# A graph layer on one core: the first gather of each group waits for TensorE, tables are moved in halves, and the sum goes first on VectorE

## The chip, the cores and the metric

The kernel runs on one core of one Trainium2 chip. The metric is the device time of one execution in microseconds. Before the change three runs gave a median of 1374.2 us (1370.36 to 1376.34).

The engines of the core are called by the names that the profile uses: PE is TensorE (matmuls; PEld is its weight loads), DVE is VectorE, ACT is ScalarE, POOL is GpSimd, and SP is SyncE, which here only issues transfers. The engines run their own instruction lists and wait for each other by semaphores.

## The reference

One message-passing layer on a graph with N = 6250 nodes of H = 128 features and E = 100000 edges with ED = 4 features each. The edges come sorted by their destination. All numbers are float32.

```python
msg_in = concatenate([x[src], x[dst], edge_attr], axis=1)      # 100000 x 260
h = silu(msg_in @ mW1 + mb1)                                   # 100000 x 128
messages = h @ mW2 + mb2
aggregated = segment_sum(messages, dst, num_segments=N)        # 6250 x 128
u = silu(concatenate([x, aggregated], axis=1) @ uW1 + ub1)
updated = u @ uW2 + ub2
y = layer_norm(x + updated, ln_g, ln_b)
out = layernorm(x + y)
```

## The kernel before, in words

**Factoring.** The first product is split by its rows: `x[src] @ mW1[:128]` is a row of the table `tab_a = x @ mW1[:128]`, and `x[dst] @ mW1[128:256] + mb1` is a row of the table `tab_b`. Both tables are made once, in an opening stage, and written to DRAM. Since the sum over edges is linear, `mW2` is applied to the nodes' sums of `h` rather than to the edges.

**Tiling.** An edge tile has P = 128 edges. G = 8 tiles make a group of GE = 1024 edges, and there are NG = 98 groups. As the edges are sorted by destination, the destinations of a group lie in a window of W = 96 consecutive nodes, whose first node is `bases[g]`. The nodes are NT = 49 tiles of 128.

**Work on one group g.** The names are those of the functions in the code.

- `fetch(g)` issues eight indirect transfers from GpSimd (L268), each of which collects 128 rows of 512 bytes by the source indices. The rows come out of `tab_a`, or, for the first RAW groups, out of `x` itself, as the table is not there yet. The buffers of the pool `gath` are AHEAD + 2 = 6, so the gathers of group g wait until the rows of group g - 6 are used.
- `load(g)` brings 96 rows of `tab_b` from the group's window into `mv`, and four rows of edge features into the lower rows of `st`. The last four rows of `mv` are the edge part of `mW1`.
- `node_matrix(g)` (L527, VectorE) writes the one-hot matrix window x edges into the upper 96 rows of `st`, and counts the edges of each node on the way.
- `products(g)` (L552, TensorE) does eight matmuls `st^T mv`. Their result `pre` (in PSUM, three buffers) is the part of `x[dst]` and of the edge features, for each edge.
- `hidden(g)` adds the gathered rows and `pre` on VectorE (the sum `s`, L570), and takes the silu on ScalarE (L571). For a raw group it turns the gathered rows of `x` on TensorE first, copies them, and multiplies them by the first half of `mW1` inside `products`.
- `edge_matrix(g)` (L540, VectorE) makes the one-hot matrix edges x window, `oh`.
- `by_nodes(g)` turns the counts (L577) and does eight matmuls `h^T oh` (L580, TensorE), which sum the hidden rows of the group by node, into the tile `held_ps`.
- `add(g)` (L586, VectorE) adds that to `acc`, features x nodes, in SBUF, and the counts to `deg`.

**Batches of nodes.** When the edges of four node tiles are complete, a `node_batch` does the rest for these nodes: two matmul stages, silu, two normalisations. It is written as a generator, and one of its steps is done at the end of each pass of the loop. There are 12 batches and one last one, about one for every eight groups.

**Order.** For SP, TensorE, VectorE and ScalarE the order of the instructions is the order of the code, by hand (`manual_schedule`). GpSimd is not in that list, and a scheduler places its gathers. In pass g the code does, in this order: `fetch(g + 4)`, `load(g + 4)`, `node_matrix(g + 3)`, `products(g + 2)`, `hidden(g)`, `edge_matrix(g + 1)`, `by_nodes(g - 1)`, `add(g - 2)`, and a step of the running batch. So on VectorE a pass is node_matrix, sum, oh, add. The tile `held_ps` is one tile for all its uses: it also holds the row of window numbers that `edge_matrix` reads. In the program as built, L577 of by_nodes(g - 1) therefore waits for `oh` of group g + 1 of the same pass, and `add(g - 2)` waits for by_nodes(g - 1) of the same pass. On VectorE the chain of a pass is then sum, oh, (by_nodes on TensorE), add, the batch's step, and the node_matrix and the sum of the next pass.

**The opening.** The gathers of the first RAW = 5 groups are issued ahead of everything else on GpSimd, 40 in number. Then the tables are made in `parts` of eight node tiles, seven parts in all, the last of one tile. For each part, TensorE turns the rows of `x` (`turn_x`) and multiplies each turned tile by the two halves of `mW1` in two calls of `product` (L322, eight matmuls of 128 columns each). VectorE moves the result of `tab_b` out of PSUM and adds the bias (L338), ScalarE moves that of `tab_a` (L341). Each is followed by a transfer of 512 KB to DRAM. The gathers of group RAW, the first from the table, wait for the transfers of all parts.

Of the kernel before, what the change touches and what calls it, by code (L numbers as in the profile page):

```python
# [8 lines left out]
F32 = mybir.dt.float32  # L9
# [9 lines left out]
P = 128  # L19
# [5 lines left out]
def kernel(  # L25
# [40 lines left out]
    nc = tc.nc  # L66
    N, H = x.shape
# [4 lines left out]
    G = 8  # L72
    GE = G * P
    NG = -(-E // GE)
# [4 lines left out]
    RB = 14  # L79
    AHEAD = 4  # L80
    LEAD = 4
    RAW = 5
    MADE = 3
    NQ = 4
    NM = 5
# [11 lines left out]
    def groups(n, g):  # L97
        return [(i, min(g, n - i)) for i in range(0, n, g)]
# [13 lines left out]
    def wide():  # L112
        return ps.tile([P, G, P], F32, name="pre", bufs=3)
# [5 lines left out]
    tpool = tables.enter_context(tc.tile_pool(name="tables", bufs=1, side="right"))  # L119
# [25 lines left out]
    x_sb = tpool.tile([P, NT, H], F32, name="x_sb")  # L145
    nf = N // P
    w1 = consts.tile([P, 2, H], F32, name="w1")
    src_l = by_group(src, 0)
    nc.scalar.dma_start(w1, mW1[: 2 * H].rearrange("(s k) f -> k s f", k=P))
    b1 = consts.tile([P, H], F32, name="b1")  # L150
# [11 lines left out]
    mv = [consts.tile([K1, H], F32, name=f"mv{k}") for k in range(NM)]  # L162
# [91 lines left out]
    tab_a = dram.tile([NP, H], F32, name="tab_a")  # L254
    tab_b = dram.tile([NW, H], F32, name="tab_b")
    ea_d = dram.tile([ED, NG * GE], F32, name="ea_d")
    near_d = dram.tile([NG, GE], U8, name="near_d")
    rows, bases, near = {}, {}, {}

    def tiles_of(g):  # L260
        return min(G, -(-(E - g * GE) // P))

    def fetch(g):
        if g >= NG:
            return
        rows[g] = gath.tile([P, G, H], F32, name="ga")
        for i in range(tiles_of(g)):
            nc.gpsimd.indirect_dma_start(  # L268
                out=rows[g][:, i, :],
                out_offset=None,  # L270
                in_=x if g < RAW else tab_a[:, :],
                in_offset=bass.IndirectOffsetOnAxis(
                    ap=src_i[:, g, i : i + 1] if g else src_0[:, i : i + 1], axis=0
                ),
            )

    for g in range(RAW):
        fetch(g)
# [30 lines left out]
    xT = consts.tile([P, NP], F32, name="xT")  # L309

    def by_node(t):
        return t[:NP].rearrange("(i p) f -> p i f", p=P)
# [2 lines left out]
    nc.vector.memset(zeros, 0.0)  # L315
    nc.sync.dma_start(tab_b[NP:NW], zeros)

    def product(i0, n, part):
        pm = wide()
        for i in range(n):  # L320
            cols = slice((i0 + i) * P, (i0 + i + 1) * P)
            nc.tensor.matmul(pm[:, i, :], xT[:, cols], w1[:, part, :], start=True, stop=True)  # L322
        return pm[:, :n]

    def turn_x(i0, n):
        pt = wide()
        for i in range(n):
            nc.tensor.transpose(pt[:, i, :], x_sb[:, i0 + i, :], ident)
        nc.scalar.copy(xT[:, i0 * P : (i0 + n) * P], pt[:, :n, :].rearrange("p i f -> p (i f)"))
# [3 lines left out]
    for k, (i0, n) in enumerate(parts):  # L333
        if k + 1 < len(parts):
            turn_x(*parts[k + 1])

        t = x_sb[:, i0 : i0 + n, :]
        nc.vector.tensor_add(t, product(i0, n, 1), b1[:, None, :].to_broadcast([P, n, H]))  # L338
        nc.sync.dma_start(by_node(tab_b)[:, i0 : i0 + n, :], t)
        t = tpool.tile([P, G, H], F32, name="t", bufs=2)  # L340
        nc.scalar.copy(t[:, :n], product(i0, n, 0))  # L341
        nc.sync.dma_start(by_node(tab_a)[:, i0 : i0 + n, :], t[:, :n])
        cols = slice(i0 * P, NW if i0 + n == NT else (i0 + n) * P)
        nc.vector.memset(acc[:, cols], 0.0)
        nc.vector.memset(deg[:, cols], 0.0)
# [23 lines left out]
    def load_weights():  # L369
        for name, shape in (("w2", [P, H]), ("u1a", [P, H]), ("mb2", [P, 1])):  # L370
            raw_w[name] = work.tile(shape, F32, name=f"raw_{name}", bufs=1)
        nc.sync.dma_start(raw_w["w2"], mW2)
        nc.sync.dma_start(raw_w["u1a"], uW1[P:])
        nc.sync.dma_start(raw_w["mb2"], mb2.rearrange("(f o) -> f o", o=1))
        nc.sync.dma_start(u1x, uW1[:P])
        nc.sync.dma_start(u2, uW2)
        nc.sync.dma_start(ub1_col, ub1.rearrange("(f o) -> f o", o=1))
        nc.sync.dma_start(ub2_row, ub2.rearrange("(o f) -> o f", o=1))
        for t, row in ((g_b, ln_g), (b_b, ln_b)):
            nc.sync.dma_start(t, row.rearrange("(o f) -> o f", o=1).to_broadcast([P, H]))  # L380

    def fuse_weights():
        pt = narrow()
        nc.tensor.transpose(pt[:, :P], raw_w["w2"], ident)
        w2T = work.tile([P, P], F32, name="w2T", bufs=1)
        nc.scalar.copy(w2T, pt[:, :P])
        pm = narrow()
        nc.tensor.matmul(pm[:, :H], w2T, raw_w["u1a"], start=True, stop=True)
        nc.tensor.matmul(pm[0:1, H:], raw_w["mb2"], raw_w["u1a"], start=True, stop=True)
        nc.scalar.copy(w2u, pm[:, :H])  # L390
        nc.scalar.copy(mb2u, pm[0:1, H:])
# [133 lines left out]
    def node_matrix(g):  # L525

        nc.vector.tensor_scalar(  # L527
            stbuf[g % NST][:W],
            near.pop(g),
            p_next,  # L530
            0.0,
            op0=OP.is_equal,
            op1=OP.add,
            accum_out=deg_g[:, g : g + 1],
        )

    def edge_matrix(g):

        oh = work.tile([P, G, W], F32, name="oh", bufs=3)
        nc.vector.tensor_tensor(  # L540
            oh,
            w_row[:, None, :].to_broadcast([P, G, W]),
            rel[:, g, :, None].to_broadcast([P, G, W]),
            op=OP.is_equal,
        )
        return oh

    def products(g, xg=None):
        pre = wide()
        st = stbuf[g % NST].rearrange("k (i c) -> k i c", i=G)  # L550
        for i in range(tiles_of(g)):
            nc.tensor.matmul(pre[:, i, :], st[:, i, :], mv[g % NM], start=True, stop=xg is None)  # L552
            if xg is not None:
                nc.tensor.matmul(pre[:, i, :], xg[:, i, :], w1[:, 0, :], start=False, stop=True)  # L554
        return pre

    def hidden(g):
        h = hbuf[g % NH]
        ga = rows.pop(g)
        if g < RAW:  # L560
            px = wide()
            for i in range(G):
                nc.tensor.transpose(px[:, i, :], ga[:, i, :], ident)
            xg = work.tile([P, G, P], F32, name="s")
            nc.vector.tensor_copy(xg, px)  # L565
            nc.scalar.activation(h, products(g, xg), AF.Silu)
        else:
            n = tiles_of(g)
            s = work.tile([P, G, H], F32, name="s")
            nc.vector.tensor_add(s[:, :n], ga[:, :n], pre.pop(g)[:, :n])  # L570
            nc.scalar.activation(h[:, :n], s[:, :n], AF.Silu)  # L571
        return h
# [19 lines left out]
    pre, oh, h, pt, running = {}, {0: edge_matrix(0)}, {}, {}, []  # L592
    for g in range(NG + 1):
        if g == 3:
            load_weights()
        if g == 5:
            fuse_weights()
        for c in range(1, NC):
            if g == max(1, c * EC // GE - 10):
                attributes(c)  # L600
            if g == max(1, c * EC // GE - 10) + 1:
                attribute_rows(c)
        if g + AHEAD >= RAW:
            fetch(g + AHEAD)
        if g + LEAD < NG:
            load(g + LEAD)
        if g + MADE < NG:
            node_matrix(g + MADE)
        if g >= RAW:
            for k in range(g if g == RAW else g + MADE - 1, min(g + MADE, NG)):  # L610
                pre[k] = products(k)
        if g < NG - 1:
            h[g] = hidden(g)
        if g + 1 < NG:
            oh[g + 1] = edge_matrix(g + 1)
        if 0 <= g - 1 < NG:
            pt[g - 1] = by_nodes(g - 1, h.pop(g - 1), oh.pop(g - 1))
        for k in range(max(g - 2, 0), g - 1 if g < NG - 1 else g):
            if k in pt:
                add(k, pt.pop(k))  # L620
        for i0, n, first in batches:
            if g == min(first + 1, NG):
                tiles = node_tiles(nodes, node_ps)
                if first == NG:

                    tiles = (
                        nodes,
                        lambda name, p=P: gath.tile([P, G, H], F32, name="ga")[:p, :BT],
                        lambda: wide()[:, :BT],
                    )  # L630
                running.append(node_batch(i0, n, *tiles))
        advance(running)
        if g >= NG - 2:
            advance(running)
        if g == NG - 1:
            h[g] = hidden(g)
# [157 lines left out]
```

## Time and profile before

The profiled execution has a span of 1372.6 us and a mean granted TensorE clock of 0.665 of full speed.

| Engine | busy us | share | instructions |
|---|---|---|---|
| PE | 704.8 | 51% | 3818 |
| DVE | 477.5 | 35% | 1012 |
| ACT | 237.4 | 17% | 288 |
| POOL | 741.4 | 54% | 790 |

| Group of instructions | count | mean ns |
|---|---|---|
| gather L268 | 742 | 946 |
| products L552 | 1564 | 336 |
| sums by node L580 | 1564 | 361 |
| node_matrix L527 | 98 | 1262 |
| sum L570 | 93 | 1204 |
| add L586 (of acc) | 98 | 255 |

| Stage | us from the start of the span |
|---|---|
| gathers of groups 0 to 4 | 4.06 to 54.15 |
| tables' work on TensorE ends | 83.5 |
| first gather from a table | 88.99 |
| sums of groups 5 to 97 | 167.98 to 1346.93 |
| last gather | 1297.96 |

A mean duration times a count is the busy time of a group of instructions. Busy time is not what sets the end where engines wait for each other, and the profile names for each group what ended the idle time before it, the releaser: "DVE s L570" is the instruction of line 570 on VectorE that writes `s`; "issue" is time without a wait that the profile shows; "remote" is a wait whose end the profile can't lay at the end of any instruction that it shows. The durations of matmuls are modelled.

### The profile page before, as it was taken

What the parts mean: (1) busy time and instruction counts of PE and PEld (TensorE: products, weight loads), DVE (VectorE), ACT (ScalarE), POOL (GpSimd) and SP (SyncE); (2) the same over time, 40 slices, a digit from 0 to 9 for tenths busy, and PEclk for the clock granted to TensorE, in tenths of its full rate; (3) what the DMA queues carried; (4) which work ended last, traced back from release to release, by engine and by line L of the source; (5) the groups of instructions that cost most, each with busy time, mean ns of one, the idle gap of its engine ahead of it and who ended that gap; (6) DMA issues with size and microseconds to landing.
All of it is one profiled execution on the core that took longest, in us unless ns stands there. A gap on an engine that the chain in (4) does not pass through costs nothing. (4 is left out here: it accounts for less than half of the span.)

```text
span 1372.6 us, 11511 instructions
## 1 busy us (share of the span) xinstructions
PE 704.8 (51%) x3818; PEld 624.6 (46%) x3818; DVE 477.5 (35%) x1012; ACT 237.4 (17%) x288; POOL 741.4 (54%) x790
## 2 busy tenths in 40 slices
PE   3356743656465355445344543675543664544565
PEld 2356643545355244345234443565433454434453
DVE  1172323324334234234233325234324333225343
ACT  0121101112212112112102201212202202202223
POOL 7435564656456556546645654666655565655400
PEclk8577775755666657656656765656756665766765
DMA  6363222212312222222212221322222222222100
GB/s 168 90 177 83 56 66 65 64 48 57 79 43 67 55 60 70 58 57 70 74 33 68 56 64 41 78 58 74 62 58 58 56 69 64 58 58 56 47 1 28
DMA packets 69917, 88.96 MB, mean 65 GB/s; under 512 B 20671, under 2 KB 51534, under 8 KB 69850
## 3 DMA queue, kind: packets, MB, share of 16 engines
q0 software_dynamic: 25024, 51.30, 15.0%
q1 hardware_dynamic: 41290, 35.08, 9.0%
q10 hardware_dynamic: 3536, 1.77, 0.5%
q8 instruction: 32, 0.52, 0.1%
q14 instruction: 35, 0.29, 0.1%
HBM read 76.71 MB, written 11.38 MB: 64 GB/s over the span
## 5 line engine op out<-in xcount | busy, mean ns | idle before, releaser
L268 POOL DMA_INDIRECT ga<-tab_a,src_i x742 | 702.2, 946 | 541.6 <-DVE s L570 277.8
L552 PE MATMUL pre<-mv,st 100*128 100x128 f32 x1564 | 278.3, 336 | 57.2 <-issue 56.9
L586 DVE TENSOR_TENSOR acc<-acc,held_ps 128x96 f32 x98 | 25.0, 255 | 780.6 <-remote 511.7
L577 PE MATMUL held_ps<-ident,deg_g 96*1 96x96 f32 x98 | 28.6, 292 | 509.6 <-DVE oh L540 482.5
L552 PEld LDWEIGHTS pre<-mv,st 100*128 100x128 f32 x1564 | 257.6, 250 | 69.2 <-issue 68.8
L580 PE MATMUL held_ps<-oh,h 128*128 128x96 f32 x1564 | 287.5, 361 | 0.3 <-ACT h L571 0.3
L580 PEld LDWEIGHTS held_ps<-oh,h 128*128 128x128 f32 x1564 | 276.6, 274 | 1.4 <-ACT h L571 0.7
L577 PEld LDWEIGHTS held_ps<-ident,deg_g 96*1 96x1 f32 x98 | 8.0, 82 | 532.3 <-DVE oh L540 501.9
L571 ACT ACTIVATE h<-s 128x1024 f32<-128x1024 f32 (+1 forms) x93 | 98.1, 1055 | 718.4 <-DVE s L570 653.3
L527 DVE TENSOR_SCALAR_CACHE_REDUCE st<-near,p_next 96x1024 f32<-96x1024 uint8 x98 | 123.5, 1262 | 24.0 <-issue 14.3
L570 DVE TENSOR_TENSOR s<-ga,pre 128x1024 f32<-128x1024 f32 (+1 forms) x93 | 112.0, 1204 | 2.9 <-PE pre L552 2.7
L540 DVE TENSOR_TENSOR oh<-held_ps,rel 128x768 f32<-128x768 f32 x98 | 92.3, 942 | 0.0
L571 ACT ACT_TABLE_LOAD x21 | 26.9, 1283 | 126.0 <-DVE s L570 113.1
L322 PE MATMUL pre<-w,xT 128*128 128x128 f32 x196 | 29.1, 307 | 31.6 <-issue 15.7
L322 PEld LDWEIGHTS pre<-w,xT 128*128 128x128 f32 x196 | 27.4, 222 | 33.5 <-issue 16.0
L268 POOL DMA_INDIRECT ga<-in_x_dram,src_i x32 | 30.3, 946 | 9.8 <-issue 9.8
L554 PE MATMUL pre<-w,s 128*128 128x128 f32 x80 | 22.1, 371 | 18.9 <-DVE s L565 16.3
L417 ACT ACT_TABLE_LOAD x24 | 30.8, 1283 | 2.7 <-DVE mv L412 2.3
L446 PEld LDWEIGHTS y<-u,uT 128*128 128x128 f32 x94 | 22.7, 327 | 15.4 <-issue 15.4
L425 ACT COPY acc_b<-acc 128x512 f32<-128x512 f32 (+1 forms) x12 | 7.3, 609 | 124.3 <-DVE acc L586 115.3
L554 PEld LDWEIGHTS pre<-w,s 128*128 128x128 f32 x80 | 17.8, 275 | 19.9 <-DVE s L565 17.0
L446 PE MATMUL y<-u,uT 128*128 128x128 f32 x94 | 26.0, 448 | 0.0
(117 smaller groups left out, 396.0 us busy)
## 6 DMA issues: line engine op xcount, KB each, us to landing
ga<-tab_a,src_i POOLq DMA_INDIRECT x742
near<-near_d SPq DMA_DIRECT2D x24, 384.0 KB
mv<-tab_b SPq DMA_DIRECT2D x98, 48.0 KB
tab_b<-x_sb SPq DMA_DIRECT2D x6, 512.0 KB
tab_a<-t SPq DMA_DIRECT2D x6, 512.0 KB
xs<-in_x_dram SPq DMA_DIRECT2D x11, 256.0 KB
out_dram<-z SPq DMA_DIRECT2D x11, 256.0 KB
st<-ea_d SPq DMA_DIRECT2D x98, 16.0 KB
```

The source lines that it names most:

```text
L268: nc.gpsimd.indirect_dma_start(out=rows[g][:, i, :], out_offset=None, in_=x if g < RAW else tab_a[:, :], in_offset=bass.IndirectOffsetOnAx ...
L322: nc.tensor.matmul(pm[:, i, :], xT[:, cols], w1[:, part, :], start=True, stop=True)
L417: nc.scalar.activation(r[:, :n], mv[:, :n, 1], AF.Sqrt, bias=eps)
L446: nc.tensor.matmul(y[:, i, :], by_p[:, :, i], u2, start=False, stop=i == n - 1)
L527: nc.vector.tensor_scalar(stbuf[g % NST][:W], near.pop(g), p_next, 0.0, op0=OP.is_equal, op1=OP.add, accum_out=deg_g[:, g : g + 1],)
L540: nc.vector.tensor_tensor(oh, w_row[:, None, :].to_broadcast([P, G, W]), rel[:, g, :, None].to_broadcast([P, G, W]), op=OP.is_equal,)
L552: nc.tensor.matmul(pre[:, i, :], st[:, i, :], mv[g % NM], start=True, stop=xg is None)
L554: nc.tensor.matmul(pre[:, i, :], xg[:, i, :], w1[:, 0, :], start=False, stop=True)
L570: nc.vector.tensor_add(s[:, :n], ga[:, :n], pre.pop(g)[:, :n])
L571: nc.scalar.activation(h[:, :n], s[:, :n], AF.Silu)
L577: nc.tensor.transpose(pt[0:1, W:], deg_g[:, g : g + 1], ident[:W, :W])
L580: nc.tensor.matmul(pt[:, :W], h[:, i, :], oh[:, i, :], start=i == 0, stop=i == n - 1)
```

## The change

There are four edits.

- **The opening's gathers.** RAW goes from 5 to 4, so the gathers of four groups, 32, come from `x`. The first gather in the code of groups 2 and 3 waits for the last matmul of the tables' parts 1 and 3 (`hold(k // 2 + 2, ins)` for k in 1 and 3). As GpSimd's order is the scheduler's, that gather stands last of the eight of its group in the program as built: 23 gathers run ahead of the first wait, 8 between the two.
- **The tables.** One matmul for each node tile makes both halves, 256 columns, with two node tiles' halves side by side. The results are moved in halves of a part: ScalarE moves `tab_a`'s, VectorE `tab_b`'s, of four node tiles each. The two transfers of a part come after both.
- **The wait in the loop.** `products(g)` of a group that is not raw records its last matmul in `made[g]`. The first gather in the code of group g waits for the products of group g - 4, if these are recorded by then, which is so from group 9 on (`fetch(8)` stands ahead of `products(4)` in the code). In the program as built that gather stands first or second of its group in most groups, further back in some. The wait adds nothing to the data that is needed; its reason is given in the code as "TensorE keeps up with the gathers".
- **VectorE's order.** `node_matrix(g + 3)` moves from ahead of the products and `hidden(g)` to behind them. A pass on VectorE is then sum, node_matrix, oh, add.

```diff
-    RAW = 5
+    RAW = 4
...
+    def hold(g, ins):
+        tc.add_manual_dep(
+            opening[g],
+            ins.ins.name,
+            mybir.DependencyInfo(mybir.DependencyClass.Sync, mybir.DependencyReason.DATA),
+            reason="TensorE keeps up with the gathers",
+        )
...
         for i in range(tiles_of(g)):
-            nc.gpsimd.indirect_dma_start(
+            ins = nc.gpsimd.indirect_dma_start(
...
+            if i == 0:
+                opening[g] = ins.ins
+                if g - AHEAD in made:
+                    hold(g, made[g - AHEAD])
...
-        t = x_sb[:, i0 : i0 + n, :]
-        nc.vector.tensor_add(t, product(i0, n, 1), b1[:, None, :].to_broadcast([P, n, H]))
-        nc.sync.dma_start(by_node(tab_b)[:, i0 : i0 + n, :], t)
-        t = tpool.tile([P, G, H], F32, name="t", bufs=2)
-        nc.scalar.copy(t[:, :n], product(i0, n, 0))
-        nc.sync.dma_start(by_node(tab_a)[:, i0 : i0 + n, :], t[:, :n])
+        tb = x_sb[:, i0 : i0 + n, :]
+        ta = tpool.tile([P, G, H], F32, name="t", bufs=2)
+        for j0, m in groups(n, G // 2):
+            pm = wide().rearrange("p (i s) f -> p i s f", s=2)
+            for j in range(m):
+                cols = slice((i0 + j0 + j) * P, (i0 + j0 + j + 1) * P)
+                ins = nc.tensor.matmul(pm[:, j], xT[:, cols], w1, start=True, stop=True)
+            own = slice(j0, j0 + m)
+            nc.scalar.copy(ta[:, own], pm[:, :m, 0, :])
+            nc.vector.tensor_add(
+                tb[:, own], pm[:, :m, 1, :], b1[:, None, :].to_broadcast([P, m, H])
+            )
+        nc.sync.dma_start(by_node(tab_b)[:, i0 : i0 + n, :], tb)
+        nc.sync.dma_start(by_node(tab_a)[:, i0 : i0 + n, :], ta[:, :n])
+        if k in (1, 3):
+            hold(k // 2 + 2, ins)
...
-            nc.tensor.matmul(pre[:, i, :], st[:, i, :], mv[g % NM], start=True, stop=xg is None)
+            ins = nc.tensor.matmul(
+                pre[:, i, :], st[:, i, :], mv[g % NM], start=True, stop=xg is None
+            )
...
+        if xg is None:
+            made[g] = ins
...
-        if g + MADE < NG:
-            node_matrix(g + MADE)
         if g >= RAW:
             for k in range(g if g == RAW else g + MADE - 1, min(g + MADE, NG)):
                 pre[k] = products(k)
         if g < NG - 1:
             h[g] = hidden(g)
+        if g + MADE < NG:
+            node_matrix(g + MADE)
```

More of the change, by code (lines that the diff above doesn't have):

```diff
@@ L257 @@
     near_d = dram.tile([NG, GE], U8, name="near_d")
-    rows, bases, near = {}, {}, {}
+    rows, bases, near, opening, made = {}, {}, {}, {}, {}
+    def hold(g, ins):
[5 more added lines that the diff above has]
+        )
     def tiles_of(g):
@@ L316 @@
     nc.sync.dma_start(tab_b[NP:NW], zeros)
[L318 to L323, printed above, removed]
     def turn_x(i0, n):
```

## The prediction

> **What bounds the kernel now.** I read the page's first parts first, then the costliest groups, then the waits, then the timeline of two passes.
>
> No engine is full: POOL is busy 54% of the span, PE 51%, DVE 35%. The slices say the same all along, so the loop is a chain that passes between engines:
>
> ```profile
> PE   3356743656465355445344543675543664544565
> POOL 7435564656456556546645654666655565655400
> ```
>
> The groups and the waits tell who waits for whom (busy us, mean ns; idle us before the group and its largest releaser; in the waits: us, times, longest):
>
> ```profile
> L268 POOL DMA_INDIRECT ga<-tab_a,src_i x742 | 702.2, 946 | 541.6 <-DVE s L570 277.8
> L586 DVE TENSOR_TENSOR acc<-acc,held_ps 128x96 f32 x98 | 25.0, 255 | 780.6 <-remote 511.7
> L577 PE MATMUL held_ps<-ident,deg_g 96*1 96x96 f32 x98 | 28.6, 292 | 509.6 <-DVE oh L540 482.5
> DVE acc L586 <- remote: 511.7, 40, 14.9
> POOL ga L268 <- DVE s L570: 277.8, 45, 10.5
> ```
>
> A gather costs GpSimd 0.946 + 0.30 us of issue = 1.25 us, so a group of 8 costs 10.0 us and 98 groups 980 us. The loop needs more: the 93 sums of L570 run from 167.98 to 1346.93 us, 1178.95 / 92 = **12.81 us per group**. The gap is GpSimd waiting 45 times for a sum, which frees the buffer of a gather. The sums wait behind the add L586 on DVE, and that 40 times for "remote", up to 14.9 us: TensorE's by_nodes. Two passes show it (start, duration, engine, line; in brackets the idle time before and its releaser):
>
> ```profile
> 719.30 0.95 DVE L540 TENSOR_TENSOR oh<-held_ps,rel 128x768 f32<-128x768 f32 x1
> 719.64 0.95 POOL L268 DMA_INDIRECT ga<-tab_a,src_i  x1 [8.77 <-DVE s L570]
> 720.41 3.62 PE L580 MATMUL held_ps<-oh,h 128*128 128x96 f32 x16
> 724.07 0.25 DVE L586 TENSOR_TENSOR acc<-acc,held_ps 128x96 f32 x1 [3.83 <-PE held_ps L580]
> 725.60 1.20 DVE L570 TENSOR_TENSOR s<-ga,pre 128x1024 f32<-128x1024 f32 x1
> 727.81 1.95 PE L580 MATMUL held_ps<-oh,h 128*128 128x96 f32 x16
> 738.42 0.95 POOL L268 DMA_INDIRECT ga<-tab_a,src_i  x1 [0.30 <-issue]
> 742.20 0.25 DVE L586 TENSOR_TENSOR acc<-acc,held_ps 128x96 f32 x1 [14.52 <-remote]
> ```
>
> The first by_nodes (720.41) is done when its row ends, 724.03. The next sum at 725.60 frees a second buffer, so GpSimd runs 16 gathers unbroken, 719.64 to 739.37. The second by_nodes starts at 727.81 and its row ends at 729.76, yet the add that waits for it starts at 742.20, 2.8 us after the last gather. Most bursts do this, the release about 3 us after the last gather, whatever the row says; in 8 of some 46 the by_nodes ended earlier, together about 45 us earlier than that. So an unbroken run of gathers longer than about 8 us holds TensorE's results back until it ends. In three bursts of a single group (312.59, 942.71, 1149.44) the by_nodes after a pause took 3.77 us; pauses of 0.95 us or less did not help.
>
> A pair of groups therefore costs: release to add 0.45, node_matrix 1.2, sum 1.14, 0.34 to the first gather, together 3.15; then 19.7 of gathers + 2.9 = 22.6. Sum 25.75 us, 12.9 per group: the loop's rate.
>
> The opening has the same mark. Forty gathers run from 4.06 to 54.15; one ACT copy waits 42.94 us and ends its wait after the last:
>
> ```profile
> 53.20 0.95 POOL L268 DMA_INDIRECT ga<-in_x_dram,src_i  x1 [0.30 <-issue]
> 60.51 1.01 ACT L341 COPY t<-pre 128x1024 f32<-128x1024 f32 x1 [42.94 <-remote]
> ```
>
> From 61.57 on, a part of the tables takes 4.45 us, until 83.5; the first gather of a table row starts at 88.99.
>
> **What the skill says.** The Trainium skill, "Perfetto Trace Analysis", section Per-instruction lifecycle, says that the end of a matmul is the profiler's estimate, "a model, not a measurement", and that the semaphore update comes after the PSUM writes are acknowledged. The trace agrees (729.76 against 742.20), so I time TensorE by who waits for it. The same page's section DMA Instruction — SWDGE says that a gather's row ends when its descriptors are written, not when its data have moved, and "DMA: Bandwidth & Descriptors", section Anatomy of one DMA, prices the fixed part of such a transfer at about 2.0 us. That TensorE is let go some 3 us after the last gather's row would fit the end of the last transfer; no page says that TensorE is held meanwhile, I have it from the trace alone, and its cause I don't know.
>
> **The change, part by part.**
>
> *1. Opening.* RAW 4 removes 8 early gathers, and two holds split the rest: 23 gathers run free (4.1 to about 33, at 1.25 each), then POOL waits for part 1's products, then 8, then for part 3's. TensorE should be let go near 33 + 3 = 36 to 39 instead of 60.5. The six further parts at 4.45 (L322's row per product halves in count but a 256-column moving operand streams as many columns; the tiles moved out are the same elements in twice as many instructions, beside PE) give 27, so the tables end near 64 to 67 instead of 83.5. Of these 17 us part is lost: groups 4, 5, 6 now all gather from the table and run on unbroken (24 x 1.25 = 30 us), which holds the first passes. I expect products(0) near 102 instead of 112: 10 us. One raw pass fewer: its transposes, copy and second product go, its gathers stay; 2 us. Together **-12**, range -5 to -22.
>
> *2. Sum ahead of node_matrix.* Node_matrix (1.26 us, L527 over 98 rows 1262 ns) stood between a late add and the sum. Now: add .45 + sum 1.14 + .34 = 1.95 instead of 3.15 to the first gather, 1.2 less per burst. 46 bursts: **-55**. Node_matrix then delays oh and by_nodes by 1.2 us; that hides, as by_nodes is held to the burst's end anyway, save in the 8 bursts where it was not.
>
> *3. The gate in the loop.* The first gather of group g also waits for products(g-4). They run in the pass of sum(g-6), which the buffer waits for already. By the semaphore events the products of the burst's second pass complete 7.6 us after its first gather in half the bursts, 9.9 to 10.7 in the others, 13 to 14 where a node batch's matmuls precede; order adds up to 1.2. The second group's first gather is due at 10.0 us. So in about half the bursts the gate is free, and the pair costs as in 2. In the others GpSimd stops after 8 gathers (behind it on its engine are only further gathers, needed four passes later), TensorE is released near 10 + 3 = 13 to 14, with it by_nodes, which was waited for until 22.7, and the next groups follow. Four groups then take about 47 us instead of 49.1 (twice 24.55, the pair after part 2): -2.1, some 12 times: **-25**.
>
> Sum: 1374.2 - 12 - 55 - 25 = **1282**.
>
> **The rivals.**
>
> *Gate breaks every burst well.* If the gate stops POOL in nearly every group, by_nodes never waits for a whole pair: 10.0 us of gathers and one release of about 1.25 (0.45 + 0.8 of the sum's lead not hidden) give 11.25 per group. 92 x (12.81 - 11.25) = 143, with the opening: 1374 - 12 - 143 = **1219**. For: a pause of 1.4 us already cleared TensorE. Against: half the products are done before the gate.
>
> *The order's gain is eaten.* TensorE's work of the second pass comes 1.2 us later and falls behind the line of 8 us; the 8 bursts whose by_nodes ended early lose their 45 us and the gate gives nothing: 1374 - 12 - 55 + 45 = **1352**. For: by_nodes' second start, 8.1 us into the burst, is near that line.
>
> *Gate waits for the release in each group (slower).* If the held products come only 3 us after the last gather, GpSimd pays that in every group: 8 gathers end 9.7 us after the first starts, 3.0, then 0.3 of issue, 13.0 to 13.2 instead of 12.81. 92 x 0.3 = 28, less 12, and without the order's gain, since the gate and not the sum starts the group: **1390**. For: products at 13 to 14 us in the batch passes do just this. Against: half come at 7.6.
>
> *The moved tables alone* can't decide more than the opening's 22 us.
>
> **Chances.** Forecast 0.47, well-broken bursts 0.22, eaten 0.17, slower 0.14. The range of eight in ten reaches from the second case's 1219, with 4 off for a longer opening gain, to 1365, above the eaten gain with the opening at its low end: **1215 to 1365**. Within 0.5% (1367 to 1381) lies only the border of two cases: 0.04. Faster 0.81, slower 0.15.
>
> **What would show it.** Right: "remote" waits of L586 under 350 us; the waits of L268 name PE's products (L552) in about half of the pairs; spacing of sums near 11.9 us; bursts of 8 beside ones of 16; first table gather near 70 us. Step 2 is right if a burst starts about 2 us after the late add. It would be wrong if TensorE stays held through shorter bursts, if the gate's wait sits in every group and lasts 3 us, or if bursts of 24 appear.

## The result and the profile after

The changed kernel takes 1314.83 us (median of 4 runs, 1308.11 to 1330.47), the kernel before 1372.28 us beside it: a ratio of **0.956** (95% interval 0.950 to 0.962); by the medians, 57 us less. The prediction had 1282 us and 92 less. The profiled execution was the longest of the four (1330.47 us); runs over 1.5% above the fastest of their kernel, as this one is, are left out of the ratios here and below. Its sums and counts show where time goes, not how much of the 57 us came from where; for that the timed experiments below are used.

The slices and the groups of the page that answer to those of before (columns as there):

```profile
PE   3737756434733553455563364445544555543665
POOL 6266666645654655566655655555655666645500
...
L277 POOL DMA_INDIRECT ga<-tab_a,src_i x750 | 707.5, 943 | 495.5 <-issue 371.7
...
L606 DVE TENSOR_TENSOR acc<-acc,held_ps 128x96 f32 x98 | 24.9, 254 | 730.7 <-remote 497.6
```

The picture is the same as before. No engine is full, and the add still waits 497.6 us for "remote" where it was 511.7. What has changed is how GpSimd waits: most of the 277.8 us for the sum `s` has become "issue", idle time for which the profile names no releaser; a gather now waits for two things. I therefore counted the stretches of gathers in the traces instead. Before, between 165 and 1250 us, 37 stretches held 16 or more gathers without a pause of 0.65 us; after, 24.

Where the wait bites, the timeline of the changed kernel looks like this:

```profile
417.31 1.95 PE L600 MATMUL held_ps<-oh,h 128*128 128x96 f32 x16
418.15 0.94 POOL L277 DMA_INDIRECT ga<-tab_a,src_i  x1 [0.30 <-issue]
420.42 0.94 POOL L277 DMA_INDIRECT ga<-tab_a,src_i  x1 [1.32 <-PE held_ps L600]
425.18 0.26 DVE L606 TENSOR_TENSOR acc<-acc,held_ps 128x96 f32 x1 [8.01 <-remote]
...
431.19 0.94 POOL L277 DMA_INDIRECT ga<-tab_a,src_i  x1 [2.34 <-remote]
```

GpSimd stops after the ninth gather of the stretch that began at 408.17, for 1.32 us, and starts again as TensorE's events arrive. The add for the by_nodes of 417.31 comes at 425.18, while the second group's gathers still run, and the next stretch begins at 431.19: 23.0 us for two groups. Where the wait does not bite, it is the old picture, with 16 gathers unbroken and an add that comes 2.7 us after the last:

```profile
272.41 0.94 POOL L277 DMA_INDIRECT ga<-tab_a,src_i  x1 [6.78 <-issue]
...
281.55 3.14 PE L600 MATMUL held_ps<-oh,h 128*128 128x96 f32 x16
...
291.13 0.94 POOL L277 DMA_INDIRECT ga<-tab_a,src_i  x1 [0.30 <-issue]
294.76 0.26 DVE L606 TENSOR_TENSOR acc<-acc,held_ps 128x96 f32 x1 [13.35 <-remote]
```

Here the second by_nodes starts at 281.55, its row ends at 284.69, and the add waits until 294.76.

### The profile page after: what moved, and what is told of

It is laid out like the page before. It is cut to its first block, busy times and chain, and to the rows that moved or that the text cites. A ratio compares the mean times of both kernels' runs of the same rounds, so it can differ in the third digit from the quotient of the medians.

```text
span 1328.6 us, 11337 instructions
## 1 busy us (share of the span) xinstructions
PE 685.9 (52%) x3696; PEld 605.2 (46%) x3696; DVE 485.2 (37%) x1018; ACT 238.9 (18%) x294; POOL 738.9 (56%) x790
## 3 DMA queue, kind: packets, MB, share of 16 engines
q10 hardware_dynamic: 3536, 1.77, 0.5%
## 4 chain that ended last, share of the span: by engine, by line
another core or an unknown queue 34%; issue 23%; DVE 21%; PE 11%; POOL 6%; DMA 3%; DVEq 1%; ACT 1%; SPq 0%; ACTq 0%; POOLq 0%
DVE st L543 7%; PE held_ps L600 6%; POOL ga L277 6%; DVE oh L556 5%; DVE s L590 2%; PE pre L568 2%; DVE z L476 1%; DVE y L473 1%; DMA ga<-tab_a,src_i 1%; DVE st L427 1%; DVE mv L428 1%; DVEq L590 1%; PE y L446 1%; DMA mv<-tab_b 1%
## 5 line engine op out<-in xcount | busy, mean ns | idle before, releaser
L606 DVE TENSOR_TENSOR acc<-acc,held_ps 128x96 f32 x98 | 24.9, 254 | 730.7 <-remote 497.6
L568 PE MATMUL pre<-mv,st 100*128 100x128 f32 x1564 | 260.6, 327 | 31.4 <-issue 31.4
L568 PEld LDWEIGHTS pre<-mv,st 100*128 100x128 f32 x1564 | 245.7, 242 | 41.5 <-issue 40.0
L591 ACT ACTIVATE h<-s 128x1024 f32<-128x1024 f32 x94 | 99.1, 1054 | 713.3 <-DVE s L590 576.8
L590 DVE TENSOR_TENSOR s<-ga,pre 128x1024 f32<-128x1024 f32 x94 | 114.4, 1217 | 28.1 <-DMA ga<-tab_a,src_i 10.7
L349 PE MATMUL pre<-w,xT 128*128 128x256 f32 x98 | 25.9, 420 | 12.9 <-DVE x_sb L352 11.7
L277 POOL DMA_INDIRECT ga<-in_x_dram,src_i x24 | 22.6, 943 | 15.6 <-PE pre L349 6.9
L572 PE MATMUL pre<-w,s 128*128 128x128 f32 x64 | 18.4, 383 | 21.0 <-DVE s L585 15.9
L349 PEld LDWEIGHTS pre<-w,xT 128*128 128x128 f32 x98 | 20.0, 211 | 17.3 <-DVE x_sb L352 13.2
L572 PEld LDWEIGHTS pre<-w,s 128*128 128x128 f32 x64 | 15.0, 289 | 21.8 <-DVE s L585 16.3
```

The source lines that it names most:

```text
L277: ins = nc.gpsimd.indirect_dma_start(out=rows[g][:, i, :], out_offset=None, in_=x if g < RAW else tab_a[:, :], in_offset=bass.IndirectOffs ...
L349: ins = nc.tensor.matmul(pm[:, j], xT[:, cols], w1, start=True, stop=True)
L568: ins = nc.tensor.matmul(pre[:, i, :], st[:, i, :], mv[g % NM], start=True, stop=xg is None)
```

## The experiments

My theory was that the parts add up: opening, order, and a wait that bites in half the cases at most. The rival was that the wait alone makes the loop's gain. The runs came to different chips, and these turned out to be of two kinds: e1 to e4 came to one chip, e5 to e8 to a second, e9, e10 and e12 to a third, e11 to a fourth. All are therefore given as ratios to the kernel before on the same chip. Where an expectation is in microseconds, I multiply the ratio by the 1374.2 us that it was reckoned from.

| Run | what it is | kernel before there, us | this, us | ratio (95%) |
|---|---|---|---|---|
| e1 | opening's edits alone | 1384.62 | 1369.7 | 0.9875 (0.983 to 0.992) |
| e2 | order alone | 1384.62 | 1350.0 | 0.9728 (0.968 to 0.978) |
| e3 | loop's wait alone | 1384.62 | 1326.38 | 0.9558 (0.950 to 0.962) |
| e4 | all but the loop's wait | 1384.62 | 1337.1 | 0.9634 (0.959 to 0.968) |
| e5 | the changed kernel again | 1021.33 | 1029.13 | 1.0068 (1.005 to 1.009) |
| e6 | every wait at its group's first gather | 1021.33 | 1030.23 | 1.0075 (1.006 to 1.009) |
| e7 | memset of 2048 columns, no wait | 1021.33 | 1177.83 | 1.152 (1.150 to 1.154) |
| e8 | memset of 512 columns, no wait | 1021.33 | 1064.93 | 1.0423 (1.041 to 1.044) |
| e9 | e7 again | 1023.19 | 1178.84 | 1.1518 (1.149 to 1.155) |
| e10 | e6 again | 1023.19 | 1029.94 | 1.007 (1.005 to 1.010) |
| e11 | before, order, memset of 2048 | 1372.94 | 1216.5 | 0.8871 (0.882 to 0.892) |
| e12 | before, order, memset of 1024 | 1023.53 | 1098.12 | 1.0724 (1.070 to 1.075) |

### One part at a time (e1 to e4)

e1 is the changed kernel with these two edits taken back:

```diff
-                if g - AHEAD in made:
-                    hold(g, made[g - AHEAD])
...
+        if g + MADE < NG:
+            node_matrix(g + MADE)
         if g >= RAW:
...
-        if g + MADE < NG:
-            node_matrix(g + MADE)
```

> The changed kernel without the loop's wait and with VectorE's old order: the opening's edits alone. In the trace of the changed kernel the sum of group 5 starts at 144.75 us, before at 167.98, 23 us earlier. Theory (the three parts add up, the order is the larger of the loop's two, the loop's wait hardly bites): about 1348 us, 1342 to 1355. Rival (the loop's wait breaks the bursts and gives the loop's gain): the same 1348. Second rival (what the opening gains is given back in the loop, since groups 4 to 6 run as one burst): 1360 to 1372.

It is 1.25% faster than before, 17 us of 1374 (10 to 24). That is 1357 us, between the ranges of the theory (1342 to 1355) and of the second rival (1360 to 1372): some of what the opening gains is lost again. In its trace the sum of group 5 starts 22.4 us earlier than in the trace of before; in the changed kernel's, 23.2.

e2 is the kernel before with the move of `node_matrix(g + MADE)` alone, the second half of that diff the other way round.

> The kernel before with node_matrix moved behind the sum, nothing else. Theory: the sum comes 1.2 us earlier after each held add, 46 pairs, less some us for the by_nodes that starts later: 1320 to 1340 us. Rival (the loop's wait gives the gain, and the order is eaten since TensorE's second by_nodes starts 1 us later in the burst): 1362 to 1375.

2.7% faster, 37 us, in the theory's range of 1320 to 1340 (1337). The order is worth something alone, so its gain is not eaten whole, but it is less than the prediction's 55. This is a late add and the next gather in before, and then in e2:

```profile
772.63 0.26 DVE L586 TENSOR_TENSOR acc<-acc,held_ps 128x96 f32 x1 [14.77 <-remote]
...
775.92 0.95 POOL L268 DMA_INDIRECT ga<-tab_a,src_i  x1 [6.37 <-DVE s L570]
```

```profile
755.67 0.25 DVE L586 TENSOR_TENSOR acc<-acc,held_ps 128x96 f32 x1 [13.36 <-remote]
...
758.05 0.94 POOL L268 DMA_INDIRECT ga<-tab_a,src_i  x1 [5.53 <-DVE s L570]
```

I took all stretches of exactly 16 gathers that start between 165 and 1250 us, 36 in before and 38 in e2. From the last add ahead of the next gather to that gather it is 2.39 us in the median instead of 3.29, and 3.43 in the mean instead of 4.58 (in some passes a step of a node batch lies between): a gain of 0.9 to 1.15 us. Part of it is lost again. The second by_nodes starts 10.2 us after the stretch's first gather instead of 8.4, and its add comes 2.25 us after the last gather in the mean instead of 1.77. Adds over 1 us ahead of the end of the gathers fell from 7 to 1. What is left is a period of 25.40 us in the mean instead of 26.09 (25.15 and 25.92 in the median).

e3 is the kernel before with `hold` and this:

```diff
+            if i == 0:
+                opening[g] = ins.ins
+                if g - AHEAD in made:
+                    hold(g, made[g - AHEAD])
...
+        if xg is None:
+            made[g] = ins
```

> The kernel before with the loop's wait on the products of group g - 4, nothing else. In the trace of the changed kernel 24 of the bursts are still of 16 gathers unbroken, and most bursts start 1.95 us after the sum's start instead of 1.48: a second wait on GpSimd costs 0.46 us there. Theory: no gain or a small loss, 1366 to 1388 us. Rival (the wait breaks the bursts): 1330 to 1350.

The theory missed, and the rival was nearly right: the wait **alone** gives 4.4%, as much as the whole change. The timeline of e3 shows how:

```profile
511.73 0.94 POOL L277 DMA_INDIRECT ga<-tab_a,src_i  x1 [2.38 <-issue]
...
519.43 1.95 PE L595 MATMUL held_ps<-oh,h 128*128 128x96 f32 x16
520.47 0.94 POOL L277 DMA_INDIRECT ga<-tab_a,src_i  x1 [0.30 <-issue]
522.75 0.94 POOL L277 DMA_INDIRECT ga<-tab_a,src_i  x1 [1.34 <-PE held_ps L595]
526.18 0.26 DVE L601 TENSOR_TENSOR acc<-acc,held_ps 128x96 f32 x1 [6.88 <-remote]
...
535.13 0.94 POOL L277 DMA_INDIRECT ga<-tab_a,src_i  x1 [2.70 <-PE held_ps L595]
535.14 0.25 DVE L601 TENSOR_TENSOR acc<-acc,held_ps 128x96 f32 x1 [5.07 <-PE held_ps L595]
```

The run of gathers breaks after eight (521.41 to 522.75). The next gather at 535.13 starts in step with the add of 535.14, not after an add, a node_matrix and a sum: its buffer had been freed by the sum of 527.98 already. So the wait gains in two ways, a break inside the pair and an earlier start of the next. In e3, 28 pauses end that way, with 2.6 us in the mean; the 46 pauses of before had 5.9. It also costs something: 28 stretches that start behind a sum start 1.9 to 2.1 us after it, where all 46 of before start 1.4 to 1.6 after it. That is 0.46 us for each, 13 us together.

e4 is the changed kernel without the three lines of the wait, the first half of e1's diff.

> The changed kernel without the wait in the loop; the opening's waits, tables and the order stay. Theory: as fast as the changed kernel or faster by up to 0.46 us for each of some 40 bursts: 1292 to 1316 us. Rival (the wait gives the loop's gain): 1335 to 1350.

3.7%, the sum of e1 and e2 (1.25 + 2.7 = 4.0) within the intervals. So the theory's time was wrong, and the rival's too. Opening and order add up; the wait on top of both is worth only 0.963 to 0.956, some 10 us, and the intervals of the two ratios, from different chips, overlap (0 to 20 us). **Alone it is worth 61, on top of the others about 10.** One reason can be read from the traces: the gains of order and wait lie in the same place, the pause between a late add and the next gather. The order makes it shorter by about 1 us, and the wait lets GpSimd start without waiting for the sum behind the add.

The place of the wait is a second difference. In e3 as built it stands at the first gather in 69 of 88 groups. In the changed kernel that holds for 35, and 33 have it at the second gather: the earlier sum frees the buffer earlier by the scheduler's reckoning, and the scheduler lets one gather through. How much of the wait's gain went to each of the two, no run separates. Nor was the opening run with the wait but without the order. If these two added up, that kernel would be at 0.9875 x 0.9558 = 0.944, an estimate from e1 and e3; the changed kernel is at 0.956, so beside the wait the order may even have cost something; the estimate's interval (0.936 to 0.952) still touches the changed kernel's.

### The place of the wait, and chips of another kind (e5 to e10)

e6 puts GpSimd's order into the hand-written ones, so that the wait stands at the first gather in every group:

```diff
-    edges.enter_context(tc.manual_schedule(engines={ENG.SP, ENG.PE, ENG.DVE, ENG.Activation}))
+    edges.enter_context(tc.manual_schedule(engines={ENG.SP, ENG.PE, ENG.DVE, ENG.Activation, ENG.Pool}))
```

e7 and e8 do that too, drop the loop's wait and break the run of gathers by an instruction that waits for nothing (2048 or 512 columns):

```diff
+    idle = consts.tile([P, 2048], F32, name="idle")
...
         rows[g] = gath.tile([P, G, H], F32, name="ga")
+        if g >= RAW + 4:
+            nc.gpsimd.memset(idle, 0.0)
```

> The changed kernel once more, on the same chip as the three that follow, for a profile to set beside theirs. Ratio to the kernel before 0.95 to 0.965; in most bursts the wait for the products stands at the second gather of its group or later.

> The changed kernel with GpSimd's order by hand as well: every loop wait then stands at the first gather of its group (in the changed kernel it stands there in 31 of 89 groups, in the kernel before with the wait alone in most), and so do the opening's two. Theory (the wait is worth what its place allows; where one to six gathers of the next group are let through first, TensorE is held longer, and the sum's earlier place made the scheduler let one through): ratio to before 0.925 to 0.945, the pauses at the wait more than in the changed kernel. Rival (the place is indifferent, order and wait just take the same slack away): 0.95 to 0.965 as the changed kernel.

> The changed kernel without the loop's wait, GpSimd's order by hand, and ahead of each group's gathers a memset of 128 x 2048 on GpSimd (some 1.7 us by the 0.20 us that one of 128 x 128 takes against 0.10 for 128 x 1), which waits for nothing. Theory (an unbroken run of gathers holds TensorE, a break of 1.4 us or more frees it): by_nodes is free after each group, the groups follow at about 12.0 us, 1265 to 1300 us. Rival (a break doesn't free TensorE, only a wait for its products does): each pair takes 1.7 to 2.0 us more than without it, 1400 to 1430 us.

> The same with a memset of 128 x 512 (some 0.5 us, 0.8 with the issue). Theory (pauses of 0.95 us or less freed nothing in the trace of before): the memset is only added, 1355 to 1385 us. Rival (any break frees TensorE): groups at about 11 us, 1190 to 1240 us.

None of this came (and the count in e6's expectation, 31 of 89, should be the 35 of 88 above). On that chip the kernel before took 1021 us, not 1380, and the changed one was 0.7% **slower**. From e5's page, and one round of its timeline:

```profile
POOL 6577777777777777777777777777777777777740
...
L606 DVE TENSOR_TENSOR acc<-acc,held_ps 128x96 f32 x98 | 24.9, 254 | 322.2 <-PE held_ps L600 322.2
```

```profile
507.16 3.62 PE L600 MATMUL held_ps<-oh,h 128*128 128x96 f32 x16
507.37 0.95 POOL L277 DMA_INDIRECT ga<-tab_a,src_i  x1 [0.30 <-issue]
...
510.82 0.26 DVE L606 TENSOR_TENSOR acc<-acc,held_ps 128x96 f32 x1 [3.83 <-PE held_ps L600]
```

GpSimd is at seven tenths from the third slice to the last but two: from 52.64 to 989.21 us the 750 gathers run without a pause of 0.65 us. Yet the by_nodes of 507.16 is answered by its add after 3.66 us, and 96 of the 97 are within 3.8 us of their start (52 of 97 within 4 us in before). A gather takes 944 ns there, about as elsewhere. So the program alone does not make the hold of TensorE: it goes with the chip, as far as the four chips of e1 to e12 show, one of them met twice. Without it GpSimd is the bound, and a wait of GpSimd for TensorE has nothing to give. e7 and e8 take 149 and 36 us more than e5, which is 90 times the memset's duration (1.82 and 0.54 us) less some 0.16 us, as it must be where GpSimd is the bound. The test of the memset and of the wait's place thus told nothing of the hold, and I repeated both.

> The kernel of the long memset once more: on the chip of the runs e5 to e8 the kernel before took 1021 us and its gathers ran without a break from the first pass to the last, so TensorE was held by nothing there and the memset could only cost. If the kernel before takes some 1380 us again in this run, the theory (a break of 1.4 us or more frees TensorE) says 0.92 to 0.95 of it, the rival (only a wait for TensorE's products does) 1.01 to 1.04. If it takes some 1021 us, both say 1.15.

> The changed kernel with GpSimd's order by hand once more, every loop wait at the first gather of its group. If the kernel before takes some 1380 us: the theory (the place of the wait decides what it is worth) says 0.925 to 0.945 of it, the rival (the place is indifferent) 0.95 to 0.965. If it takes some 1021 us, both say 1.007.

The second chip was of the same kind (1023 us), and both ratios came out as said for it. What the place of the wait is worth where TensorE is held was not measured.

### A break that waits for nothing, where TensorE is held (e11)

The kernel before, order moved, GpSimd's order by hand, memset of 2048 columns from group 8 on:

> The kernel before, its opening too, with node_matrix behind the sum, GpSimd's order by hand, and the memset of 128 x 2048 on GpSimd ahead of each group's gathers from group 8 on. If the kernel before takes some 1380 us in this run: the theory (a break of 1.4 us or more frees TensorE) has groups at 11.7 to 12.0 us instead of the 12.6 of the order alone, 1280 to 1300 us, 0.925 to 0.94 of before; the rival (a break alone doesn't) has one memset more inside each of 46 pairs, 1410 to 1430 us, 1.02 to 1.035. If it takes some 1021 us, where GpSimd never waits for TensorE: the opening's edits are what made the changed kernel 8 us slower there, by 8 gathers less that lie ahead of the tables; with the old opening this kernel is 8 us faster than the same with the new one, 1.144 of before against 1.152. If instead the order or the loop's wait cost the 8 us, it stays at 1.152.

This chip is of the kind that holds TensorE (before 1372.94 us), and 90 memsets of 1.82 us made the kernel **156 us faster**, 0.887 of before, where the order alone was 0.973. It is beyond the theory's range on its own side, and 0.13 from the rival's. Its page, waits and timeline:

```profile
POOL 6506768788887878878788787887878878788760
...
L590 DVE TENSOR_TENSOR acc<-acc,held_ps 128x96 f32 x98 | 24.9, 255 | 384.4 <-PE held_ps L584 227.4
```

```profile
DVE acc L590 <- remote: 31.1, 4, 8.3
```

```profile
700.40 1.82 POOL L270 MEMSET idle<- 128x2048 f32 x1
702.03 1.22 DVE L574 TENSOR_TENSOR s<-ga,pre 128x1024 f32<-128x1024 f32 x1 [4.18 <-DMA ga<-tab_a,src_i]
702.38 0.95 POOL L272 DMA_INDIRECT ga<-tab_a,src_i  x1 [0.16 <-issue]
...
705.48 3.62 PE L584 MATMUL held_ps<-oh,h 128*128 128x96 f32 x16
709.14 0.26 DVE L590 TENSOR_TENSOR acc<-acc,held_ps 128x96 f32 x1 [3.83 <-PE held_ps L584]
```

The add waits for "remote" 31.1 us in 4 times, instead of 511.7 in 40. The by_nodes of 705.48, in the middle of a group's gathers, is answered after 3.66 us, and 89 of the 97 within 4 us, where it was 52 in before. The sum now waits for the landing of gathers, 4.18 us here: GpSimd has become the bound, 8 x 1.25 us of gathers and 1.68 more for the memset (a break of 1.98 instead of 0.30), 11.68 us for a group. So long unbroken runs of gathers are what holds TensorE's results on such a chip, and a break of 1.98 us after every eight gathers, which nobody waits for, prevents it.

The length of a break is not all that counts, though. The trace of before has one of 1.85 us that comes after 16 gathers:

```profile
877.80 0.94 POOL L268 DMA_INDIRECT ga<-tab_a,src_i  x1 [1.85 <-issue]
878.56 3.62 PE L580 MATMUL held_ps<-oh,h 128*128 128x96 f32 x16
...
890.42 0.26 DVE L586 TENSOR_TENSOR acc<-acc,held_ps 128x96 f32 x1 [12.03 <-remote]
```

The by_nodes behind it was held until 2.9 us after the last of the next eight gathers. Breaks of 1.90 us (e1), 2.25 (e2) and 2.17 (e4) after 16 gathers did not free the next by_nodes either. What lies ahead of the break seems to count too; no run varied it.

On this kind of chip e11's kernel beats the changed kernel (0.887 against 0.956). GpSimd's order by hand, which came with the memset, was not run alone on it; where TensorE is not held, it changed nothing (e5 and e6). On the other chips the same memset costs 15%, so no version here is best on both.

### Half the break (e12)

The kernel of e11 with 1024 columns.

> The kernel of e11 with a memset of half the size, 128 x 1024: between the 543 ns of 512 columns and the 1824 ns of 2048 it takes about 0.97 us, and the break between two gathers is about 1.1 us instead of 1.98. If the kernel before takes some 1380 us in this run: if a break of 1.1 us frees TensorE too, groups at 10.8 us, 1140 to 1155 us, 0.83 to 0.845 of before; if it doesn't (pauses of 0.95 us or less did not in the trace of before), one memset more in each pair than with the order alone, 1375 to 1395 us, 0.995 to 1.01. If before takes some 1021 us: a memset cost its duration less 0.16 us in e7 and e8, here 0.81 x 90 = 73 us; with the old opening 1021 + 73 = 1094 us, if the opening's edits made the changed kernel 8 us slower there, and 1102 if the order or the wait did.

The chip was one without the hold, so whether 1.1 us would do stays open. For the second question, whether the new opening is at fault for the 8 us on such a chip, it took 1098.12 us, between the 1094 that say yes and the 1102 that say no. With 972 ns measured for the memset, and before at 1023.53, the two work out at 1023.53 + 90 x 0.812 = 1096.6 and 1104.6, and the measured time is nearer the first. That points to the opening's edits, and the timelines show why. This is e5, the new opening, at its first gather from the table:

```profile
52.64 0.94 POOL L277 DMA_INDIRECT ga<-tab_a,src_i  x1 [8.49 <-DMA mv<-in_L_gnn_mW_dram]
```

and this e12, the old one:

```profile
54.91 0.94 POOL L272 DMA_INDIRECT ga<-tab_a,src_i  x1 [0.30 <-issue]
```

With 40 gathers ahead of it GpSimd never waits for the tables there; with 32 it waits 8.49 us. e12's is the 41st gather; the 41st of e5 starts at 62.62 us, 7.7 us later. The changed kernel was 7.8 us slower than before on e5's chip.

## Why the prediction came out as it did

The direction and the range were right, the size of the gain was not: 92 us forecast, 57 measured.

- **What bounds the kernel.** That long runs of gathers hold TensorE back, and that this, not any engine's work, sets the loop's rate, was read from the trace of before alone. e11 bore it out: with the runs broken, the hold was all but gone and the time fell by 11%, order included. What I could not see from one chip's trace is that other chips do not do it. The pause of 1.4 us that "already cleared TensorE" is not in that trace: the shortest one that did so there is 2.35 us, and one of 1.85 us did not.
- **Step 1, the opening.** -12 forecast, -17 measured (e1), in its range of -5 to -22. The first gather from the table came at 67.25 us (forecast near 70), and then 24 gathers ran without a break, 67.25 to 96.89. The tables' work on TensorE ended at 59.2 us, though, not at 64 to 67, and products(0) was done by 88.6 us instead of 111.8, 23 us earlier and not the forecast's 10. What the forecast took off ahead of products(0) was lost behind it, in the loop.
- **Step 2, the order.** -55 forecast, -37 measured (e2). The saving between the late add and the next gather was near, 0.9 in the median and 1.15 us in the mean instead of 1.2. The term mis-sized was what node_matrix's delay of by_nodes costs. I had put it at nothing "save in the 8 bursts" and then left those 8 out of the sum; it took 0.48 us of each stretch in the mean. The 0.69 us that are left, 46 times, make 32 us.
- **Step 3, the wait.** -25 forecast on top of the others. Alone it gave -61 (e3), on top about -10, 0 to -20 by the intervals (e4 against the changed kernel). **This is the step that failed.** Its count, that the wait bites in some half of the pairs, was near: 28 pauses in e3, 23 in the changed kernel. It put the cost of a second wait on a gather at nothing, and that is 0.46 us at each of 23 starts behind a sum in the changed kernel, some 11 us. It also lacked that the wait replaces the chain from the add to the next gather, which step 2 had already sold; this is read from the traces and not separated by a run. That the scheduler moved the wait behind other gathers in 53 of 88 groups stands in neither sum; its share was not measured.
- **The rivals.** "Order's gain eaten" was refuted by e2, which gained, though some 0.48 of 1.15 us was eaten. "Breaks every burst well" did not happen with this wait, since 24 of the stretches stayed unbroken; e11, which does break every one, reaches 1216.5 us. That this is near the rival's 1219 is chance: the rival's sum has the new opening and no memset. The slower rival is refuted where TensorE is held. On the chips where it is not, the change is slower by 0.7%, but, as e12 points to, for the opening and not for that rival's reason.
- **What would show it.** "Remote" waits under 350 us was wrong (497.6), and so was a spacing of the sums near 11.9 us (12.54 in the profiled execution, 12.29 in e3). The waits of the gathers name the products only 3 times. The first gather from the table and, in e2, the starts 2 us after a late add were right (2.39 us in the median).

Open are the cause of the hold, what distinguishes the chips that show it, how long a break must be after how many gathers, and what the place of the wait is worth.

## What to carry to other kernels

Two edits that shorten the same pause are not worth their sum: ask for each which wait it takes away, and price the second on the kernel that has the first. A wait that carries no data was worth 4% here because it paced an engine whose unbroken work held another's results back, and a plain pause was worth 11% together with the order. The row end of a matmul in the profile did not show the hold; the instruction that waited for it did. Before tuning against such an effect, look at a second chip.

## What was not expected of the hardware

- On the chips where before took 1365 to 1395 us, unbroken gathers held TensorE's results, mostly until 2.7 to 3.3 us after the last gather. On two others the same program took 1021 to 1024 us in the median, and in e5 the adds waited 97 times for TensorE, 322.2 us in all, and never for "remote". Gathers took 943 to 949 ns on both. The Trainium skill, "Perfetto Trace Analysis", section Per-instruction lifecycle, lets the semaphore update follow the modelled end of a matmul; here the add came 0.04 us after that end on one kind of chip (510.78 to 510.82 in e5) and 10.07 us after it on the other (284.69 to 294.76 in the changed kernel).
- A break of 1.98 us in every group, at 1.82 us of GpSimd's time each, made a kernel with the new order 156 us faster than before on one kind of chip; with the new opening too, the same memset made it 156 us slower than before on the other kind.
- Breaks of 1.85 to 2.25 us after 16 gathers freed nothing, while 1.98 us after every eight did.
- A second wait on a gather moved the start of a stretch from 1.4 to 1.6 us after the sum to 1.9 to 2.1 us.
